# A mixture-of-experts tail in a two-layer decoder: outputs in a row per choice, w1 and w3 loaded per tile, the last batch in two parts

## The chip, the cores and the metric

The kernel runs on one core of a Trainium2 chip. The metric is the time of one execution on the device in microseconds (us); several runs are made, and their median counts. Of one further execution there is a hardware profile with every instruction's start and duration. The engines are TensorE (PE; its weight loads are listed apart as PEld), VectorE (DVE), ScalarE (ACT), GpSimd (POOL) and SyncE (SP), which only issues transfers here. SP and POOL issue DMA transfers to 16 shared DMA engines.

## The reference, cut to what matters

The input is x of 4 batches by 256 tokens by 256 features, and a context of 4 by 1601 by 256. Two layers follow each other, each with self-attention, cross-attention and a feed-forward part, and each part ends with a residual and a layer norm. Layer 0 has a sliding window, softmax attention over the context, and a ternary feed-forward part. Layer 1 has causal attention (16 heads over a compressed key), a gated linear attention over the context, and a mixture of experts, which is where the change lies:

```python
x = x + moe(x); out = layernorm(x)

def moe(x):                                   # x: 1024 tokens x 256
    logits = 30 * tanh((x @ w_gate) / 30)     # 8 experts
    probs = softmax(logits)
    idx = top_k(probs, 2)
    weights = probs * one_hot(idx).sum(-2)
    out = 0
    for e in range(8):
        h = silu(x @ w1[e]) * (x @ w3[e])     # 256 -> 512 inner units
        out += (h @ w2[e]) * weights[:, e]    # 512 -> 256
    return out
```

All is float32. Only two of eight experts count for a token, so the kernel sorts tokens by expert and computes only those.

## The kernel before, in words

The program isn't written in the order in which it runs. Each operation is recorded with the data it reads and writes, an estimated duration and a priority; then a planner (`Loom.weave`, L301) takes, again and again, the operation that can start earliest by its estimates, and writes it out. So the order on every engine is fixed when the program is built, by estimated times (`LAT` and the `us` of each operation), by the number of buffers of each kind, and by `at_prio`. At run time each engine follows its own list in order, and waits where the data aren't there. Almost every instruction is recorded by a helper, so the profile has the helper's line: L253 for matmuls, L260 for transposes, L382 for DVE, ACT and POOL operations, L267 for plain transfers. The tile names tell them apart. [...]

The main loop (L1464) goes over the four batches b: `l1_attention(b)`, `l1_cross(b)`, then `route(b)`. Tokens are handled in tiles of 128 (two per batch). After three batches the first tables of expert tiles are made, and their tiles may start while the fourth batch is still being worked on. Routing and experts work as follows.

- `moe_prepare` (L1176) fills the DRAM table `lists` with padding. Each expert has 1024 places in it, each place two numbers: gate and token. It zeroes `xd` and `acc`, two DRAM copies of x with spare rows.
- `route(b)` (L1227) writes x of the batch to `xd` and to `acc`, computes the gate (`wgate`), picks the two best, finds each token's place in its expert's list with five small matmuls against a triangular and an all-ones matrix (`ahead`, `onesb`: the rank), and scatters the entries with four indirect transfers on POOL (`enter`, L1212, `lists<-entry`).
- `tile_table(n, taken)` (L1287) computes on DVE which expert and which 128 rows of `lists` each of the next n tiles has. `EARLY` is 5 (the full tiles that must exist after three batches), `LATE` is 18 (all that can be left). Places that no token took are padding, and their rows go to spare rows.
- `expert_tile(i, tab)` (L1337) does one tile of 128 rows. SP reads the row number from the table and fetches the entries (`mine<-lists`, L1346). POOL gathers the 128 rows of x (`xg<-xd`, L1349). PE transposes them (2 transposes, `xgT`). Then xgT is the stationary side and w1, w3 (`w`, a slice of `w13` picked by a register) the moving side: 4 matmuls of 512 columns into two banks. ACT takes tanh of the first and DVE multiplies up to `eh`, 128 tokens by 512 units. PE transposes eh (4 transposes, `ehT`), multiplies with w2 (4 matmuls of 256 columns), DVE applies the gate (`ey`), and POOL adds the rows into `acc` in DRAM with an indirect transfer that adds (`acc<-ey`, L1357).
- At the end each batch's rows of `acc` are read back (L1482), normalised and written to `out`.

A float32 matmul is two instructions in the profile, each with a weight load of its own; a float32 transpose is one. Weights w1, w3 of all experts (8.4 MB) are loaded once into `w13` by 16 transfers, w2 (4.2 MB) once into `w2e`. The order of the adds into `acc` comes from the framework: two transfers that write the same DRAM tensor wait for each other unless they are declared independent, as the `enter` scatters are.

Of the kernel before, what the change touches and what calls it, by code (L numbers as in the profile page):

```python
# [175 lines left out]
class Loom:  # L176
# [62 lines left out]
    @contextmanager  # L239
    def piece(self, us, claims=(), ins=(), what=""):  # L240

        self.cur = ([], [], list(ins))
        yield
        fns, outs, ins = self.cur
        self.cur = None
        self.op({"PE": (us, us, lambda: [f() for f in fns])}, outs, ins, claims, what=what)
# [54 lines left out]
    def weave(self):  # L301
# [11 lines left out]
        while left:  # L313
# [22 lines left out]
            if op.size is not None:  # L336
                self.free["DMA"] = max(self.free["DMA"], at + us) + op.size / self.RATE
                op.end, op.engine = self.free["DMA"] + op.land, "DMA"
# [70 lines left out]
def decoder(ctx: ExitStack, tc: tile.TileContext, a: dict, out: bass.AP):  # L409
# [23 lines left out]
    down = scope("left", [even], on=experts)  # L433
# [15 lines left out]
    p6w, p6d = experts.pool("p6w"), down.pool("p6d")  # L449
# [138 lines left out]
    def normalise(x):  # L588
        mv = tiny((P, 2, 2), "mv")
        for t in range(2):  # L590
            st = tiny((P, 6), "st")
            k.vector.bn_stats(st, x[:, t, :])
            k.vector.bn_aggr(mv[:, t, :], st)
        rstd = tiny((P, 2), "rstd")
        k.gpsimd.tensor_scalar(rstd, mv[:, :, 1], 1e-5, None, ALU.add)
        k.gpsimd.tensor_tensor(rstd, rstd, mhalf, ALU.pow)
        for t in range(2):
            k.vector.tensor_scalar(
                x[:, t, :], x[:, t, :], mv[:, t, 0:1], rstd[:, t : t + 1], ALU.subtract, ALU.mult
            )  # L600

    def norm(b, x):

        normalise(x)
        xt = xpool.tile((P, 2, S), F32, "xt")
        ps = bank((P, 2, 2, P))
        for t in range(2):
            with piece(0.22, [xt], what="norm"):
                for c in range(2):
                    turn(ps[:, c, t, :], x[:, t, c * P : (c + 1) * P], ident)  # L610
        evac(xt.rearrange("p c (t q) -> p c t q", t=2), ps)
        X[b], XT[b] = x, xt
# [12 lines left out]
    def project_out(pool, x_new, t, x_old, o, wo, gate=None):  # L625
# [8 lines left out]
        else:  # L634
            k.vector.scalar_tensor_tensor(oT, gate[:, :, t * P : (t + 1) * P], 1.0, pt, ALU.add, ALU.mult)
# [16 lines left out]
    def l0_attention(b):  # L652
# [11 lines left out]
        for i in range(3):  # L664
            pv = bank((P, D))
            with piece(0.86, what="v"):
# [67 lines left out]
    def feature_map(pool, dst, ps, n, width, bufs=2):  # L734

        e = pool.tile((P, 512), F32, "fm", bufs=bufs)[:n, :width]
        k.scalar.activation(e, ps, AF.Exp)
# [314 lines left out]
    def l1_attention(b):  # L1052
# [16 lines left out]
        def four(q4):  # L1069

            ps = project_in(XT[b], lambda c, j: m_w[:, c, 2 * q4 + j, :], [qeT], "q")
            evac(qeT[:, 2 * q4 : 2 * q4 + 2, :], ps)
            aT0 = pool.tile((P, 2, 2, S), F32, "aTa")
            aT1 = pool.tile((P, 2, 2, P), F32, "aTb")
            for t in range(2):
# [4 lines left out]
                with piece(0.65 if t == 0 else 1.15, [at, aT0, aT1], what="scores"):  # L1080
# [15 lines left out]
                for kc in range(t + 1):  # L1096
# [4 lines left out]
                    dst = aT0[:, :, :, t * P : (t + 1) * P] if kc == 0 else aT1  # L1101
                    evac(dst, pt.rearrange("p (u i) q -> p u i q", u=2))

            po = bank((P, 2, S))
            with piece(1.42, what="pv"):
                for u in range(2):
                    half = slice(64 * u, 64 * u + 64)
                    mm(po[half], ctk[:, 0, :], aT0[:, u], True, False, skip_group_check=True)
                for u in range(2):
                    half = slice(64 * u, 64 * u + 64)  # L1110
                    mm(po[half, :, P:], ctk[:, 1, :], aT1[:, u], False, True, skip_group_check=True)
            evac(qeT[:, 2 * q4 : 2 * q4 + 2, :], po)

        for q4 in range(4):
            four(q4)
        xn = new_x()
        for t in range(2):
            py = bank((P, D))
            with piece(3.46, [xn], what="out"):
                for i in range(8):  # L1120
                    mm(py, qeT[:, i, t * P : (t + 1) * P], w2o[:, i, :], i == 0, i == 7)
            k.vector.tensor_tensor(xn[:, t, :], py, X[b][:, t, :], ALU.add)
        norm(b, xn)


    def l1_cross(b):
        pool = p5
        qf = pool.tile((P, 2, S), F32, "qf", bufs=1)
        pq = project_in(XT[b], lambda c, j: wqg[:, 0, c, j * P : (j + 1) * P], [qf], "q")
        feature_map(pool, qf.rearrange("p j q -> p (j q)"), pq.rearrange("p j q -> p (j q)"), P, 512, 1)  # L1130

        gate = pool.tile((P, 2, S), F32, "gate", bufs=1)
        pg = project_in(XT[b], lambda c, j: wqg[:, 1, c, j * P : (j + 1) * P], [gate], "gate")
        for j in range(2):
            k.scalar.activation(gate[:, j], pg[:, j], AF.Tanh, bias=bg[:, j : j + 1], scale=0.5)
        xn = new_x()
        for t in range(2):
            pn = bank((P, H, 17))
            o = pool.tile((P, H, 16), F32, "o")
            with piece(0.47, [o], what="kvs"):  # L1140
                for j in range(2):
                    mm(
                        pn[:, 8 * j : 8 * j + 8, :].rearrange("p h e -> p (h e)"),
                        qf[:, j, t * P : (t + 1) * P],
# [9 lines left out]
            project_out(pool, xn, t, X[b], o.rearrange("p h e -> p (h e)"), wxo, gate)  # L1154
        norm(b, xn)
# [8 lines left out]
    EARLY = -(-(2 * 3 * S - NE * (P - 1)) // P)  # L1164
    LATE = 2 * T // P + NE - 1 - EARLY
# [6 lines left out]
    lists = in_dram((LISTS, 2), "lists", I32)  # L1172
    xd = in_dram((T + P, D), "xd")
    acc = in_dram((T + P, D), "acc")

    def moe_prepare():  # L1176
# [9 lines left out]
        pad = tmp.tile((P, n, 2), I32, "pad", bufs=1)  # L1186
        k.gpsimd.memset(pad, 0)
        k.gpsimd.tensor_copy(pad[:, :, 1], w)
# [368 lines left out]
```

## Time and profile before

| | us |
|---|---|
| median of 3 runs (lowest, highest) | 734.64 (733.61, 734.69) |
| the profiled execution | 731.26 |
| its span, first to last instruction | 729.5 |
| PE busy in the span | 672.8 |
| DVE, ACT, POOL busy | 438.5, 302.6, 158.3 |
| expert tiles on PE, first to last | 551 to 708 |

The span is shorter than the execution's time by what lies before the first and after the last instruction. In the page's row of forty slices one slice is 18.2 us, and a digit is the busy share in tenths. PE is counted busy while matmuls are in flight, so its share tells where it stands still, and not how well it is used. [...] the pace is read from the distance between starts: 0.43 us for an instruction of 512 columns, 0.216 for 256, 0.109 for a transpose of 128. The DMA share is that of 16 engines, and GB/s what they moved.

### The profile page before, as it was taken

The numbers are of one execution on the slowest core, as the hardware profiler recorded it, in microseconds if no ns is written. First come the engines' busy times: TensorE is split into PE (matmuls) and PEld (weight loads), VectorE is DVE, ScalarE is ACT, GpSimd is POOL, SyncE is SP. The second block draws the span as 40 slices with busy tenths as digits, with TensorE's granted clock in tenths as the row PEclk, the third lists the DMA queues.
The fourth block names the chain that finished last, engine by engine and source line by source line (L and its number), as shares of the span: only waits on it lengthen the run. The fifth ranks groups of instructions, "written<-read, shape, count | busy, mean of one in ns | idle before, by whom it ended". The sixth has DMA issues, their size and how long they took to land.

```text
span 729.5 us, 11204 instructions
## 1 busy us (share of the span) xinstructions
PE 672.8 (92%) x3920; PEld 490.8 (67%) x3920; DVE 438.5 (60%) x1067; ACT 302.6 (41%) x931; POOL 158.3 (22%) x190
## 2 busy tenths in 40 slices
PE   7999999999999999999899999999977959999970
PEld 5778787678867786767676777777654635665640
DVE  4899886334493535665999877887754513333323
ACT  2868664211232224343467765656611202222210
POOL 3220324022100000000121010303122456522232
PEclk9999999999999999999999999999999989999995
DMA  9901212538632230000203900003601143312214
GB/s 307 341 18 59 92 35 87 173 128 273 219 115 91 91 122 1 1 0 1 53 1 115 347 1 30 1 30 62 199 2 37 30 56 90 59 21 23 23 22 123
DMA packets 51819, 63.39 MB, mean 87 GB/s; under 512 B 7758, under 2 KB 41684, under 8 KB 51764
## 3 DMA queue, kind: packets, MB, share of 16 engines
q1 hardware_dynamic: 46836, 56.63, 23.9%
q0 software_dynamic: 4928, 6.05, 5.3%
q8 instruction: 32, 0.52, 0.3%
q14 instruction: 23, 0.19, 0.1%
HBM read 54.05 MB, written 8.61 MB: 86 GB/s over the span
## 4 chain that ended last, share of the span: by engine, by line
PE 73%; DVE 13%; DMA 5%; ACT 4%; issue 2%; POOL 1%; SPq 0%; POOLq 0%; DVEq 0%; ACTq 0%
PE bank L253 65%; PE bank L260 8%; DVE at L382 3%; ACT at L382 3%; DMA acc<-ey,mine 2%; DVE nm L382 2%; DVE x L382 2%; DVE h L382 1%; DVE as L382 1%; DMA lists<-entry,rowi 1%; DMA xg<-xd,mine 1%; DVE st L382 1%; DMA x<-acc 1%; POOL rstd L382 1%; DMA wqkv<-in_wqkvT 0%
## 5 line engine op out<-in xcount | busy, mean ns | idle before, releaser
L382 ACT ACTIVATE at<-at,nm 128x128 f32<-128x128 f32 (+1 forms) x256 | 106.3, 418 | 23.5 <-DVE nm L382 22.9
L253 PE MATMUL bank<-w,xgT 128*128 x184 | 85.0, 608 | 0.5 <-ACT xgT L382 0.5
L260 PE MATMUL bank<-ident,at 128*128 128x128 f32 (+1 forms) x440 | 60.4, 275 | 1.1 <-DVE at L382 0.4
L253 PEld LDWEIGHTS bank<-w,xgT 128*128 128x128 f32 x184 | 35.0, 197 | 37.1 <-issue 36.0
L260 PEld LDWEIGHTS bank<-ident,at 128*128 128x128 f32 (+1 forms) x440 | 50.7, 141 | 13.0 <-issue 4.8
L382 POOL TENSOR_SCALAR rstd<-mv 128x2 f32<-128x2 f32 x24 | 6.3, 263 | 244.2 <-DVE mv L382 226.1
L253 PE MATMUL bank<-V,aT 128*128 128x256 f32 (+1 forms) x240 | 55.2, 380 | 1.4 <-DVE o L382 1.4
L253 PE MATMUL bank<-KT,qT 128*128 128x512 f32 (+1 forms) x128 | 53.8, 554 | 0.0
L253 PEld LDWEIGHTS bank<-V,aT 128*128 128x128 f32 (+1 forms) x240 | 45.0, 190 | 11.6 <-issue 4.4
L1357 POOL DMA_INDIRECT acc<-ey,mine x23 | 36.1, 1569 | 72.7 <-DVE ey L382 42.1
L253 PE MATMUL bank<-kf,V 128*128 128x256 f32 (+1 forms) x208 | 49.9, 382 | 1.1 <-DVE kf L382 1.1
L382 DVE TENSOR_REDUCE nm<-at 128x4 f32<-128x512 f32 x64 | 50.7, 809 | 0.5
L253 PE MATMUL bank<-wkv,KT 128*128 128x256 f32 (+1 forms) x208 | 49.7, 383 | 0.0
L382 ACT ACTIVATION_READ_ACCUMULATOR at<-at,nm 128x1 f32 x256 | 48.4, 189 | 0.0
L253 PE MATMUL bank<-w2e,ehT 128*128 x184 | 43.9, 385 | 2.9 <-ACT ehT L382 2.8
L382 POOL TENSOR_TENSOR at<-at,rs 128x512 f32<-128x512 f32 (+1 forms) x17 | 20.3, 1191 | 111.0 <-DVE rs L382 70.0
L253 PEld LDWEIGHTS bank<-kf,V 128*128 128x128 f32 (+1 forms) x208 | 38.5, 190 | 7.7 <-DVE kf L382 2.3
L382 ACT COPY aT<-bank 128x512 f32<-128x512 f32 (+2 forms) x57 | 29.1, 540 | 33.3 <-PE bank L260 33.0
L253 PEld LDWEIGHTS bank<-wkv,KT 128*128 128x128 f32 (+1 forms) x208 | 37.7, 186 | 7.5 <-issue 1.9
L253 PEld LDWEIGHTS bank<-w2e,ehT 128*128 128x128 f32 x184 | 34.0, 190 | 12.3 <-ACT ehT L382 4.4
L382 DVE TENSOR_TENSOR at<-at,rs 128x512 f32<-128x512 f32 (+1 forms) x47 | 39.2, 834 | 1.0
L382 ACT ACTIVATE eh<-bank 128x512 f32<-128x512 f32 x23 | 13.7, 597 | 59.4 <-PE bank L253 59.4
(248 smaller groups left out, 1252.0 us busy)
## 6 DMA issues: line engine op xcount, KB each, us to landing
w<-in_w SPq DMA_DIRECT2D x16, 512.0 KB, 9.3
KT<-in_ctxT SPq DMA_DIRECT2D x6, 1024.0 KB, 6.2
V<-in_ctx SPq DMA_DIRECT2D x6, 1024.0 KB, 7.5
w2e<-in_w SPq DMA_DIRECT2D x8, 512.0 KB, 9.4
KT<-in_ctxT SPq DMA_DIRECT2D x6, 577.0 KB, 4.7
V<-in_ctx SPq DMA_DIRECT2D x6, 512.0 KB, 4.1
wq<-in_w1qT SPq DMA_DIRECT2D x8, 256.0 KB, 4.8
wo<-in_w1o SPq DMA_DIRECT2D x8, 256.0 KB, 3.1
```

Of the source, the lines that this page charges most:

```text
L253: lambda: self.nc.tensor.matmul(real(o), real(lhsT), real(rhs), start=real(start), stop=stop, **kw)
L260: fns.append(lambda: self.nc.tensor.transpose(real(o), real(x), real(ident)))
L382: return getattr(engine, method)(*[real(x) for x in args], **{k: real(x) for k, x in kw.items()})
L1357: nc.gpsimd.indirect_dma_start(out=acc.real(), out_offset=bass.IndirectOffsetOnAxis(ap=ids.real(), axis=0), in_=y.real(), in_offset=None, ...
```

## The change

- An expert's output isn't added in DRAM any more. `yd` has a row for each token and choice (2 x 1024 rows, and one for each padding place). An entry of `lists` has a third number, that row. `expert_tile` scatters `ey` to those rows (`scatter`, called "give"), and the transfers are declared independent of each other. `acc` is gone. x stays in SBUF, and at the end each batch reads two blocks of `yd` (`back`, four buffers) and adds them to x on DVE before it is normalised.
- The inner units lie on the rows: w1 and w3 are the stationary side, in pieces of 128 units, and xgT the moving side, 128 columns. The result is h with units on the partitions, which is what the w2 matmul needs, so the four transposes and their evacuation go.
- w1 and w3 of a tile's expert are loaded for each tile, by SP with a register from the table, into one of four buffers (`wt`). `w13` and its 16 loads are gone; w2 stays loaded once, and its pool no longer waits for the attention's pool, so it comes earlier.
- `EARLY` becomes a list: 5 tiles after three batches and 2 more after the first half of the last batch; `LATE` becomes 16. For that the last batch goes through `l1_attention`, `l1_cross` and `route` in two halves of 128 tokens; `l1_attention` is a generator that yields after each half. The scatter of a half's entries is two transfers.
- `piece` gets an argument `over`: the matmuls of layer 0's v wait in the plan for the earlier readers of the v buffer they are evacuated to. The planner's estimate for small transfers (under 0.3 MB) changes. Both alter the order only.

The diff, cut to its core:

```diff
-    def piece(self, us, claims=(), ins=(), what=""):
+    def piece(self, us, claims=(), ins=(), over=(), what=""):
...
+        read = [o for v in over for _, o in v.buf.reads]
+        self.op({"PE": (us, us, lambda: [f() for f in fns])}, outs, ins, claims, after=read, what=what)
...
-                self.free["DMA"] = max(self.free["DMA"], at + us) + op.size / self.RATE
-                op.end, op.engine = self.free["DMA"] + op.land, "DMA"
+
+                begin, took = at + us, op.size / self.RATE
+                self.free["DMA"] = max(self.free["DMA"], begin) + took
+                if op.size < 0.3:
+                    behind = self.free["DMA"] - took > begin
+                    op.end = min(self.free["DMA"], begin + (2 * took + 1.0 if behind else took)) + op.land
+                else:
+                    op.end = self.free["DMA"] + op.land
+                op.engine = "DMA"
...
-    EARLY = -(-(2 * 3 * S - NE * (P - 1)) // P)
-    LATE = 2 * T // P + NE - 1 - EARLY
+    EARLY = [-(-(2 * n - NE * (P - 1)) // P) for n in (3 * S, T - P)]
+    EARLY[1] -= EARLY[0]
+    LATE = 2 * T // P + NE - 1 - sum(EARLY)
...
-    lists = in_dram((LISTS, 2), "lists", I32)
+    lists = in_dram((LISTS, 3), "lists", I32)
     xd = in_dram((T + P, D), "xd")
-    acc = in_dram((T + P, D), "acc")
+    yd = in_dram((2 * T + LISTS, D), "yd")
...
+    def scatter(dst, row, src, us, land, what):
+
+
         def emit():
             k.hold_order(False)
             d = nc.gpsimd.indirect_dma_start(
-                out=lists.real(),
+                out=dst.real(),
                 out_offset=bass.IndirectOffsetOnAxis(ap=row.real(), axis=0),
-                in_=entry.real(),
+                in_=src.real(),
                 in_offset=None,
             )
-            tc.declare_no_dep(d.ins, group="entries", reason="no two of them have a row in common")
-            tc.add_to_no_dep_group("entries", d.ins)
+            tc.declare_no_dep(d.ins, group=what, reason="no two of them have a row in common")
+            tc.add_to_no_dep_group(what, d.ins)
...
-        def add_up():
-            nc.gpsimd.indirect_dma_start(
-                out=acc.real(),
-                out_offset=bass.IndirectOffsetOnAxis(ap=ids.real(), axis=0),
-                in_=y.real(),
-                in_offset=None,
-                compute_op=ALU.add,
-            )
...
+        def weights():
+            expert(nc.sync)
+            for j, w in enumerate(("w1", "w3")):
+                nc.sync.dma_start(
+                    out=wt.real()[:, j],
+                    in_=a[w][bass.ds(reg[nc.sync], 1), :, :].rearrange("o (c p) n -> p (o c) n", p=P),
+                )
+
+        entry = p5.tile((P, 3), I32, "mine", bufs=LATE)
         k.op({"SP": (1.1, 1.1, fetch)}, [entry], [lists, tab], size=0.05, land=2.2, what="fetch")
-        ids, gate = entry[:, 1:2], entry[:, 0:1].bitcast(F32)
-        xg = pool.tile((P, D), F32, "xg", bufs=10)
+        wt = p6w.tile((P, 2, 2, EI), F32, "wt", bufs=4)
+        k.op({"SP": (1.6, 1.6, weights)}, [wt], [tab], size=8e-6 * D * EI, what="weights")
+        gate, ids, slots = entry[:, 0:1].bitcast(F32), entry[:, 1:2], entry[:, 2:3]
+        xg = p5.tile((P, D), F32, "xg", bufs=6)
...
-        with piece(3.45, [h], ins=[w13], what="tile"):
+
+        h = pool.tile((P, EI // P, P), F32, "eh")
+        pa = [bank((P, EI // P, P)), bank((P, EI // P, P))]
+        with piece(3.52, [h], what="tile"):
             for j in range(2):
-                for c in range(2):
-                    mm(
-                        pa[j], xgT[:, c, :], lambda j=j, c=c: w13.real()[:, bass.ds(reg["e"], 1), j, c, :].squeeze(1),
-                        c == 0, c == 1,
-                    )
+                for m in range(EI // P):
+                    for c in range(2):
+                        mm(pa[j][:, m], wt[:, j, c, m * P : (m + 1) * P], xgT[:, c, :], c == 0, c == 1)
...
-        hT = pool.tile((P, 4, P), F32, "ehT")
-        ph = bank((P, 4, P))
-        with piece(0.44, [hT], what="tile"):
-            for c in range(4):
-                turn(ph[:, c, :], h[:, c * P : (c + 1) * P], ident)
-        evac(hT, ph)
...
-        k.op({"POOL": (1.65, 1.65, add_up)}, [acc], [y, ids], size=0.13, what="add up")
+        scatter(yd, slots, y, 1.0, 2.0, "give")
...
-    w13 = p6w.tile((P, NE, 2, 2, EI), F32, "w13")
-    for e in range(NE):
-        k.dma_start(w13[:, e, 0], rows(a["w1"][e]))
-        k.dma_start(w13[:, e, 1], rows(a["w3"][e]))
-    w2 = p6d.tile((P, NE, 4, D), F32, "w2e")
+    w2 = p6w.tile((P, NE, 4, D), F32, "w2e")
...
     for b in range(B):
         at_prio(7, b)
-        l1_attention(b)
-        at_prio(6, b)
-        l1_cross(b)
-        if b == B - 1:
-            at_prio(8)
-            tab, taken = tile_table(EARLY, None)
-            for i in range(EARLY):
-                expert_tile(i, tab)
-        at_prio(6, b)
-        route(b)
+        for ts, x, xt in l1_attention(b):
+            at_prio(6, b)
+            if ts[0] == 0:
+                xn, xnt = p5.tile((P, 2, D), F32, "xl", bufs=B), new_xt()
+            l1_cross(b, ts, x, xt, xn, xnt)
+            if b == B - 1:
+                at_prio(8)
+                n = EARLY[ts[0]]
+                tab, taken = tile_table(n, taken)
+                for i in range(n):
+                    expert_tile(i, tab)
+            at_prio(6, b)
+            route(b, ts, xn, xnt)
+            at_prio(7, b)
+        X[b] = xn
     at_prio(8)
-    tab, _ = tile_table(LATE, taken)
+    tab, _ = tile_table(LATE, taken, True)
     for i in range(LATE):
         expert_tile(i, tab)
     for b in range(B):
-        x = new_x()
-        k.dma_start(x, acc[b * S : (b + 1) * S, :].rearrange("(t p) d -> p t d", p=P))
+        x = X[b]
+        for e in range(2):
+            y = p6.tile((P, 2, D), F32, "back", bufs=4)
+            row0 = e * T + b * S
+            k.dma_start(y, yd[row0 : row0 + S, :].rearrange("(t p) d -> p t d", p=P))
+            k.vector.tensor_tensor(x, x, y, ALU.add)
         normalise(x)
```

The core of the split in `l1_attention` is this loop, where the earlier kernel has `four(q4)` for both halves at once:

```python
        for ts in ((0,), (1,)) if b == B - 1 else ((0, 1),):
            for q4 in range(4):
                four(q4, ts)
            ...
            norm_into(xn, xt, ts)
            yield ts, xn, xt
```

## The prediction

> **What bounds the kernel now.** I read the page first (busy shares, the forty slices), then the chain that ended last, then tables by stage of the last third, and last the timelines of PE and POOL there.
>
> ```profile
> PE 672.8 (92%) x3920; PEld 490.8 (67%) x3920; DVE 438.5 (60%) x1067; ACT 302.6 (41%) x931; POOL 158.3 (22%) x190
> PE   7999999999999999999899999999977959999970
> DMA  9901212538632230000203900003601143312214
> ```
>
> PE is the bound nearly everywhere: 73% of the chain is PE work, and up to 533 us PE lacks only some 16 us, 5 of them waiting for the first weights. So a gain must shorten PE's own work or fill its holes. Two holes are left: slices 29 to 32 (529 to 602 us) and the last one and a half. The table by stage places them. Columns: window, its length, busy us (instructions) of PE, PEld, DVE, ACT, POOL, granted clock, DMA share, GB/s.
>
> ```profile
> 400.00:404.00 4.00, 4.00 (x26) 2.75 (x24) 3.79 (x7) 2.83 (x11) 0.00 (x0) 1.00 1.05 386
> 585.00:590.00 5.00, 3.23 (x16) 2.31 (x14) 1.26 (x3) 0.59 (x1) 1.34 (x1) 1.00 0.53 26
> 590.00:595.00 5.00, 0.00 (x0) 0.00 (x0) 0.00 (x0) 0.00 (x0) 2.58 (x2) 0.86 0.31 27
> 595.00:600.00 5.00, 3.09 (x5) 1.47 (x6) 0.00 (x0) 0.37 (x1) 3.24 (x3) 0.50 0.40 65
> 610.00:700.00 90.00, 89.56 (x337) 56.24 (x336) 29.70 (x49) 20.58 (x41) 31.44 (x24) 1.00 0.24 35
> 706.00:730.00 24.00, 1.99 (x8) 1.44 (x8) 6.86 (x25) 0.06 (x1) 6.57 (x10) 0.65 0.36 99
> ```
>
> From 610 to 700 PE is full: the expert tiles are purely PE-bound. Around 590 it stands still and then runs at half clock. What it waits for (start, duration, engine, line, operation, idle time before and its releaser):
>
> ```profile
> 586.91 1.99 PE L253 MATMUL bank<-w2e,ehT 128*128 x8 [0.68 <-ACT ehT L382]
> 596.45 0.66 PE L260 MATMUL bank<-ident,xg 128*128 128x128 f32 x2 [7.54 <-DMA xg<-xd,mine]
> 597.57 5.08 PE L253 MATMUL bank<-w,xgT 128*128 x8 [0.46 <-ACT xgT L382]
> 584.75 1.59 POOL L1357 DMA_INDIRECT acc<-ey,mine  x1 [0.30 <-DVE eh L382]
> 591.48 1.56 POOL L1357 DMA_INDIRECT acc<-ey,mine  x1 [5.14 <-DMA acc<-ey,mine]
> 593.34 1.02 POOL L1349 DMA_INDIRECT xg<-xd,mine  x1 [0.31 <-issue]
> ```
>
> The last batch's routing (rank matmuls at 577.6) must be scattered to the lists, land, be fetched and gathered before a late tile can start at 596.5, 19 us later; five early tiles don't cover it. POOL makes it worse: each add into acc waits for the add before, and the gathers queue behind.
>
> [...]
>
> ```profile
> 197.01 0.53 PEld L253 LDWEIGHTS bank<-wkv,gT 128*128 128x128 f32 x4
> 197.46 0.53 PEld L253 LDWEIGHTS bank<-ones,kacc 128*128 128x128 f32 x4
> ```
>
> Four loads in 0.45 us, 0.112 each, with 128 moving columns behind each, and 0.11 even with one column. [...] here it was granted 0.50 after 7.5 us, and that w pass took 5.08 us where a warm one takes 3.60. [...]
>
> **The change part by part.** The sum is against the profiled execution's 731.3 us.
>
> 1) *Units on the rows.* A tile on PE now: 2 transposes 0.22; w1 and w3 as 8 instructions of 0.43 (3.44); 4 transposes of eh 0.44; w2 8 x 0.216 = 1.73: 5.83 us. (17 w passes and 18 of everything else make 101 us; 604 to 705 is 101.) After, w1/w3 are the stationary side: 16 matmuls of 128 columns, two passes each, 32 x 0.111 = 3.55, and the four transposes and their evacuation (0.59 us, mostly on ACT) go: 5.50 us. 23 tiles x 0.33 = **-7.6 us**. [...]
>
> 2) *The last batch in two parts, 5+2 early and 16 late tiles.* PE's columns stay the same: causal attention and l1_cross work on 128 rows twice instead of 256 once. Extra small instructions on DVE, ACT and POOL hide under PE; DVE is 24 of 33 us busy from 500 to 533. In the built order of the changed kernel the last rank matmul is followed on PE by 3 w1/w3 blocks after its own tile's w2 chain: w2 x5 (8.6), w x3 (10.6), transposes: about 20 us before the first late gather is needed. The chain it covers shrinks: two scatters instead of four (-2.5) and no add to wait for, some 16 us, plus 2 for queueing. Its SP order has a cost: a weight load that waits for a free buffer, then the fetch. So the hole goes: 0.68 + 7.54 + 0.46 + 0.66 us idle and 1.5 slow = **-10.8 us** (bounds: -11 to 0).
>
> 3) *Weights per tile.* Each tile loads 1.05 MB, 24 MB in all instead of 8.4 once. The 400 to 404 row moved the same w1/w3 rows at 386 GB/s: 2.7 us per tile against 5.5 of PE, with four buffers, so in steady state it hides. SP needs about 1.05 us for a fetch and 1.6 for two loads with their register read (0.5 each when not held up): 2.7 of 5.5. If the cover went, a tile would run at DMA's pace. At the start it doesn't hide: fetches 1 to 4 stand behind weight loads, so I follow the order. With the third batch's rank done at 0, first rows are at PE at 17.4 as now (533.3 to 550.7); tile 2's rows, needed early in tile 1, come at about 25.5 where PE is ready at 24.7; tile 4's gather stands on POOL behind a give (which needs ey of tile 0, at 31.3) and two list scatters, and lands at 38.7 where PE asks at 37.3. The lists of part one land at 40.5, the next fetch follows. **+2.5 us** for these stalls (0 to +10). Loads of w2 move earlier, into the quiet 390 to 420: nothing.
>
> 4) *Rows in yd.* Scatters carry no wait on each other. In steady state the adds were hidden (PE full), so nothing but what 2) took. SP loses the waits on acc.
>
> 5) *The end of PE.* Now from the last w pass (701.6) to the last ey (starts 708.15) is 6.5 us, with two idle bits before w2. After: tanh 0.6, two DVE steps of 0.69 and hops, 2.4 us, then 1.73 and 0.2: 4.4. Of the 2.1 saved, 0.9 are transposes counted in 1): **-1.2**.
>
> 6) *The tail.* Now:
>
> ```profile
> 708.15 0.48 DVE L382 TENSOR_SCALAR ey<-bank,mine 128x256 f32<-128x256 f32 x1 [2.68 <-PE bank L253]
> 710.20 1.55 POOL L1357 DMA_INDIRECT acc<-ey,mine  x1 [2.91 <-DMA acc<-ey,mine]
> 713.95 1.92 SPq L267 DMA_DIRECT2D x<-acc  x4
> 716.63 0.76 DVE L382 BATCH_NORM_STATS2 st<-x 128x6 f32<-128x256 f32 x2 [8.00 <-DMA x<-acc]
> ```
>
> Last ey at 708.6, end at 729.5: 20.9 us. After: issue 0.3; scatter 3.6 (unseen; a gather lands in 2.8, an add in 3.8: bounds 2.8 to 5.4, a list scatter's median); SP 0.4; first row block 2.7; DVE, 7.7 us from 716.6 to 724.3, now with eight adds of 128x512 (0.68 us for such a step at 512.8) = 5.4 more, minus some 0.8 of gaps they fill; then 5.2 from the last DVE step to the end. 24.5: **+4.0** rounded up for eight loads through four buffers (bounds +1 to +6).
>
> 7) *The rest.* A planner lays out the whole program, and `over` and a new DMA estimate change its order from the first layer on. With PE nearly full there, I take 0, -4 to +4.
>
> Sum: -7.6 -10.8 +2.5 -1.2 +4.0 = -13.1, so 718.2 for a profiled execution. The profiled one was 3.4 under the median of its runs (734.64), so the median after: **721.6 us**.
>
> **Rivals.** *The hole stays* (15%): the late weight load heads SP's queue, waits for tile 3's buffer, and with scatters behind gathers on POOL the chain again outlasts the seven early tiles. For it: SP and POOL are strictly in order here, as 591.48 shows. Against: about 4 us of slack by my count. Price: the 10.8 comes back in the main: 728 to 733 us.
>
> *Better than that* (14%): the start stalls vanish and the tail's adds hide under landing loads; 2.5 + 3 less, and 2 to 3 from a better early order: 711 to 714.
>
> *The weights become the bound* (12%): gathers, gives and fetches share the engines, and the tile's pace becomes its 1.05 MB. Against: 386 GB/s seen, four buffers. It decides from 5.50 + 13.1/23 = 6.07 us per tile, 173 GB/s, on; at 150 GB/s a tile takes 7.0 and the kernel gets 34 us longer: about 756 us. A landing time doubled by contention with the buffer freed late would do the same.
>
> *It doesn't do what it says* (under 1%): gives still in series. The built order shows no wait of one give on another's landing.
>
> **How the numbers follow.** Forecast 57%, 714 to 728 us; rivals as above; 2% no change. About 0.2% is what a measurement of this kernel can tell from none, so faster means under 733.2: 57 + 14 + 14 (the standing hole, nearly all of it) = 85%; within 2%; slower 13%. The range leaves out the weights case and the outer edges: 711 to 732. The forecast's own: 714 to 728.
>
> **What would show it.** w1/w3 in 32 passes of 0.11 us and a tile period of 5.5 (step 1); no PE wait over 2 us on xg between the early and late tiles, clock 1.0 there (2); small waits on xg or wt in the first four tiles, and wt landing under 8 us (3); no wait of a give on a give (4); last ey to end about 25 us, DVE busy 12 of it (6). A PE wait on wt in the steady stage, or passes over 0.125 us, would make the prediction wrong.

## The result, and the profile after

| | before | after |
|---|---|---|
| median us (lowest to highest, runs) | 734.21 (733.61 to 734.69, 4) | 746.29 (745.44 to 749.01, 4) |
| the profiled execution, its span | 731.26, 729.5 | 749.01, 747.2 |

After/before is 1.0179, 95% interval 1.0159 to 1.0199: 1.8% slower. 721.6 us was predicted; it is 25 us more, and on the other side. The profiled executions differ by 17.7 us of span, where the working had -13.1: 30.8 us are to be found.

The page of after, its busy PE and the slices of PE and of the transfers (18.7 us each):

```profile
PE 677.9 (91%) x4407; PEld 539.0 (72%) x4411; DVE 447.8 (60%) x1118; ACT 292.3 (39%) x916; POOL 152.8 (20%) x199
PE   5899899999999999999899899999976888999960
DMA  9910121436732341000100600000003648776424
```

The digits where the prediction looked (the last ten) aren't much worse than before. The first is: 5 where it was 7. Two milestones, read from the first and last start of a tile's instructions, split the span: the last matmul of layer 0's feed-forward part (`wq,hqT`), and the last `ey` on DVE. Between them PE's time is split by two-us windows of the stage table: not busy is idle; busy times one minus the granted clock is what the lower clock costs; the rest is work.

| us | before | after |
|---|---|---|
| start to the last `wq,hqT` | 393.7 | 409.0 |
| of it idle / lost to the clock | 11.6 / 0.0 | 19.6 / 6.0 |
| from there to the last `ey` | 314.4 | 312.7 |
| of it work | 285.9 | 277.7 |
| of it idle / lost to the clock | 23.7 / 4.8 | 24.2 / 10.9 |
| last `ey` (its start) to the end | 21.4 | 25.5 |

So 15.3 of the 17.7 us arise in layer 0, before the attention, routing and experts of layer 1 that the change is about; 4.1 are the tail; the middle, where 8.2 us of work went, won only 1.7.

**The early part.** The timeline of PE, after, and the stage table of the same microseconds, before and then after (columns as in the prediction):

```profile
12.58 1.33 PE L255 MATMUL bank<-kT,qT 32*128 32x256 f32 x24
19.82 6.50 PE L255 MATMUL bank<-xt,wqkv 128*128 128x256 f32 x16 [5.91 <-DMA xt<-in_xT]
```
```profile
14.00:19.00 5.00, 5.00 (x43) 3.88 (x36) 4.01 (x8) 2.34 (x11) 0.00 (x0) 1.00 1.09 354
19.00:27.00 8.00, 6.83 (x56) 4.98 (x55) 6.50 (x15) 6.63 (x29) 2.35 (x3) 1.00 1.07 390
```
```profile
14.00:19.00 5.00, 0.00 (x0) 0.00 (x0) 4.83 (x8) 0.00 (x0) 0.00 (x0) 0.97 1.09 363
19.00:27.00 8.00, 7.18 (x20) 5.88 (x21) 0.75 (x1) 3.39 (x16) 0.00 (x0) 0.59 1.07 389
```

After, PE stands 5.91 us for the transposed x of the second batch, and then does its 16 matmuls in 6.50 us, 0.41 each where a warm one of 256 columns takes 0.216: 20 instructions in eight us where before had 56. A second wait that before doesn't have follows: 2.05 us at 35.29, for `at` on POOL.

**The tiles, the late rows and the tail** (steady stage, timeline of PE there and at the first late tiles, and the last `ey` with what follows on its chain):

```profile
640.00:715.00 75.00, 75.00 (x571) 71.87 (x570) 25.55 (x42) 12.11 (x27) 23.31 (x25) 1.00 0.63 213
723.00:747.00 24.00, 0.00 (x0) 0.00 (x0) 11.46 (x32) 0.00 (x0) 5.30 (x9) 0.55 0.44 137
```
```profile
644.86 7.31 PE L255 MATMUL bank<-xgT,wt 128*128 128x128 f32 x64
661.41 7.31 PE L255 MATMUL bank<-xgT,wt 128*128 128x128 f32 x64
...
604.88 0.43 PE L262 MATMUL bank<-ident,xg 128*128 128x128 f32 x2 [0.28 <-DMA xg<-xd,mine]
633.32 0.44 PE L262 MATMUL bank<-ident,xg 128*128 128x128 f32 x2 [2.21 <-DMA xg<-xd,mine]
```
```profile
721.67 0.48 DVE L391 TENSOR_SCALAR ey<-bank,mine 128x256 f32<-128x256 f32 x1 [1.24 <-PE bank L255]
722.43 0.96 POOL L1258 DMA_INDIRECT yd<-ey,mine  x1 [0.77 <-DVE ey L391]
724.97 6.97 SPq L269 DMA_DIRECT2D back<-yd  x8
727.79 1.50 DVE L391 TENSOR_TENSOR xl<-xl,back 128x512 f32<-128x512 f32 x2 [5.63 <-DMA back<-yd]
```

Three tiles take 661.41 - 644.86 = 16.55 us, 5.52 each, with PE 100% busy while the transfers, the tiles' weights among them, move 213 GB/s. The wait of 7.54 us for the late rows is gone; 2.21 is the longest one left. From the end of the last `ey` (722.15) to the end are 25.0 us, and DVE is busy 11.5 of the last 24, where the prediction had 12.

**The middle.** What it won at 585 to 600 it lost again in waits that before doesn't have (PE, after):

```profile
423.84 1.06 PE L262 MATMUL bank<-ident,at 128*128 128x128 f32 x8 [2.47 <-ACT at L391]
...
542.53 1.06 PE L262 MATMUL bank<-ident,at 128*128 128x128 f32 x8 [1.13 <-DVE mv L391]
544.85 1.11 PE L262 MATMUL bank<-ident,xl 128*128 128x128 f32 x4 [1.25 <-DVE xl L391]
...
564.88 1.08 PE L262 MATMUL bank<-ident,at 128*128 128x128 f32 x4 [2.87 <-DVE upto L391]
579.62 0.41 PE L262 MATMUL bank<-ident,x 128*128 128x128 f32 x2 [2.81 <-DVE upto L391]
```
```profile
545.00:547.00 2.00, 2.00 (x10) 1.45 (x12) 1.66 (x3) 1.00 (x4) 0.00 (x0) 0.50 0.39 131
566.00:574.00 8.00, 6.90 (x25) 5.17 (x26) 3.85 (x26) 1.93 (x5) 1.53 (x2) 0.50 0.13 26
```

No wait here is over 3 us, and yet each group of them is followed by some us at a clock of 0.50 (426 to 428, 545 to 547, 566 to 574 and 582 to 584 us). The largest group lies in the last batch, whose second half stands behind DVE: `upto` is a step of the tile table, in DVE's queue among the softmax of the half batch.

### The profile page after: what moved, and what is told of

Same layout as the page of the kernel before. It is cut to its first block, busy times and chain, and to the rows that moved or that the text cites. A ratio compares the mean times of both kernels' runs of the same rounds, so it can differ in the third digit from the quotient of the medians.

```text
span 747.2 us, 12375 instructions
## 1 busy us (share of the span) xinstructions
PE 677.9 (91%) x4407; PEld 539.0 (72%) x4411; DVE 447.8 (60%) x1118; ACT 292.3 (39%) x916; POOL 152.8 (20%) x199
## 4 chain that ended last, share of the span: by engine, by line
PE 74%; DVE 10%; DMA 5%; POOL 3%; issue 3%; SPq 2%; ACT 2%; POOLq 0%; DVEq 0%; ACTq 0%
PE bank L255 66%; PE bank L262 9%; DVE at L391 4%; SPq L269 2%; DVE nm L391 2%; POOL lists L1258 1%; ACT at L391 1%; DMA xg<-xd,mine 1%; POOL rstd L391 1%; DMA xt<-in_xT 1%; DMA trig<-in_rope 1%; DMA back<-yd 1%; DVE xl L391 1%; DVE x L391 1%; DVE st L391 0%
## 5 line engine op out<-in xcount | busy, mean ns | idle before, releaser
L255 PE MATMUL bank<-xgT,wt 128*128 128x128 f32 x736 | 87.1, 279 | 0.5 <-ACT xgT L391 0.5
L255 PEld LDWEIGHTS bank<-xgT,wt 128*128 128x128 f32 x736 | 86.6, 196 | 1.3 <-ACT xgT L391 0.7
L391 POOL TENSOR_SCALAR rstd<-mv 128x2 f32<-128x2 f32 (+1 forms) x26 | 8.4, 322 | 218.1 <-DVE mv L391 190.2
L391 DVE TENSOR_REDUCE nm<-at 128x4 f32<-128x512 f32 (+1 forms) x64 | 50.5, 809 | 0.3
L391 POOL TENSOR_TENSOR at<-at,rs 128x512 f32<-128x512 f32 (+1 forms) x18 | 22.5, 1250 | 129.3 <-DVE rs L391 114.8
L391 ACT COPY aT<-bank 128x512 f32<-128x512 f32 (+2 forms) x59 | 29.9, 544 | 37.7 <-PE bank L262 37.4
L255 PE MATMUL bank<-w2e,eh 128*128 x184 | 43.3, 380 | 0.0
L391 DVE SCALAR_TENSOR_TENSOR eh<-eh,bank 128x512 f32<-128x512 f32 x23 | 15.8, 686 | 36.2 <-ACT eh L391 36.2
L1258 POOL DMA_INDIRECT yd<-ey,mine x23 | 22.7, 985 | 71.0 <-DVE ey L391 55.7
```

The source lines that it names most:

```text
L255: lambda: self.nc.tensor.matmul(real(o), real(lhsT), real(rhs), start=real(start), stop=stop, **kw)
L391: return getattr(engine, method)(*[real(x) for x in args], **{k: real(x) for k, x in kw.items()})
L1258: d = nc.gpsimd.indirect_dma_start(out=dst.real(), out_offset=bass.IndirectOffsetOnAxis(ap=row.real(), axis=0), in_=src.real(), in_offset= ...
```

## The experiments

Ratios are to the kernel before, run beside each kernel on the same chip; 0.1% is 0.73 us. The medians of before itself range from 731.2 to 736.0 us over the chips used, so verdicts go by ratios and the traces are read for places. "Order" means here all that the planner decides: the order on each engine, and also the engine itself for some copies and products (thr02 has 1114 instructions on DVE and 920 on ACT, iota2 1109 and 925).

### Is the early loss the planner's estimate?

The new estimate treats every transfer under 0.3 MB as one that needn't wait its turn: `begin + 2 x took + 1.0 + land`, with 0.262/0.25 = 1.05 and a `land` of 1.6, 4.7 us after its issue. That covers the gathers of 0.13 MB, and also the x loads of 0.262 MB. In the run, the second batch's x was issued at 12.06 us behind the context's loads, and PE got it at 19.82, 7.8 later. The context's loads were issued from 3.34 us on, before this one, and the transfers moved 363 GB/s from 14 to 19 us; what held the x back among them the trace doesn't name. By its estimate the planner put this batch's matmuls right behind the first batch's scores, and the context's first keys (`wkv,KT`) after them, although their data were there: thr02 runs them at 13.55 without a wait. Three kernels: thr02 moves the bound,

```diff
-                if op.size < 0.3:
+                if op.size < 0.2:
```

est_old takes the estimate of before for all sizes and keeps `over`:

```diff
-                begin, took = at + us, op.size / self.RATE
...
+                self.free["DMA"] = max(self.free["DMA"], at + us) + op.size / self.RATE
+                op.end, op.engine = self.free["DMA"] + op.land, "DMA"
```

and before_est_new is the kernel before with the new estimate (bound 0.3) and `over`, and nothing else of the change.

> The changed kernel, with one number changed: the planner's new estimate for transfers holds under 0.2 MB instead of 0.3, so it still covers the gathers and scatters of 0.13 MB and no longer the 0.26 MB loads of x and of weights at the start. No instruction is added or removed; only the order is laid out anew. Theory A (step 7 failed: with the bound at 0.3 the planner believes that batch 1's x lands early, puts its q, k, v matmuls fifth on PE, and PE stands 5.9 us for x there and starts cold): the first layer-0 cross-attention matmul comes at about 186 instead of 198.7, and the time is 10 to 15 us lower, 731 to 736. Theory B (the early loss has nothing to do with the estimate; it comes from other pools or the wait of the v matmuls, argument over): within 3 us of the changed kernel's 746.

> The changed kernel with the planner's estimate for transfers as it was before the change, for all sizes; the argument over stays. Theory A: the early part is as in the run with the bound at 0.2 MB, first layer-0 cross-attention matmul at about 186; the expert part, whose order the estimate was made for, may be laid out worse: 731 to 740. Theory B: 746, as the changed kernel.

> The kernel before, with the planner's new estimate (bound 0.3 MB) and the argument over, and nothing else of the change: the same instructions in another order. Theory A: it loses by itself what the changed kernel loses early, first layer-0 cross-attention matmul at about 198 instead of 185.9, and the time is 10 to 18 us over the kernel before: 744 to 752. Theory B: 734, as before.

| | ratio (95%) | first `wqk` matmul | last `wq,hqT` |
|---|---|---|---|
| before | 1 | 185.9 | 393.7 |
| after | 1.0179 (1.0159 to 1.0199) | 198.7 | 409.0 |
| thr02 | 1.0054 (1.0036 to 1.0073) | 186.1 | 394.6 |
| est_old | 1.0094 (1.0061 to 1.0126) | 186.3 | 394.9 |
| before_est_new | 1.0165 (1.0128 to 1.0202) | 196.9 | 403.9 |

PE in thr02, and in before_est_new, in the same place:

```profile
13.55 5.45 PE L255 MATMUL bank<-wkv,KT 128*128 128x256 f32 x24
20.12 1.99 PE L255 MATMUL bank<-kf,V 128*128 128x256 f32 x8 [1.12 <-DVE kf L391]
```
```profile
19.66 5.67 PE L254 MATMUL bank<-xt,wqkv 128*128 128x256 f32 x15 [4.62 <-DMA xt<-in_xT]
```

Theory A stands from both sides: one number undoes the early loss (14.4 us to the last `wq,hqT`, 1.25% of the time), and the planner's edits alone, put into the kernel before, bring it: 1.65%, nearly as much as the whole change. est_old keeps `over` and has no early loss, so `over` isn't its cause. What is left in thr02's span are 4.0 us of tail and 0.9 early, of which the middle, 311.8 us long, gives back 2.6. est_old isn't better than thr02, so no harm of the new estimate for the 0.13 MB gathers shows; one order of each can't exclude it.

### What the split is worth

```diff
-for ts in ((0,), (1,)) if b == B - 1 else ((0, 1),):
+for ts in ((0, 1),):
-EARLY = [... for n in (3 * S, T - P)]
+EARLY = [... for n in (3 * S,)]
```

> The changed kernel without its last batch in two parts: one pass of 256 tokens, 5 early and 18 late tiles as in the kernel before; the rest stays, the early order too. Theory C (splitting costs more in front of the tiles, in DVE work and a longer way from rank to first rows, than the hole it fills): the way from the third batch's rank to the first rows falls from 25 to about 17, the hole before the late tiles is back (8 to 11 us), and the time is within 3 us of the changed kernel's 746. My step 2 as predicted (splitting is worth 10.8 and costs nothing): about 755 to 757.

1.0319 (1.0291 to 1.0346): 1.4% or 10.3 us over after. In this order theory C falls, and step 2's 10.8 for the split was about right. But the hole it fills isn't the 7.54 us of before (PE, then SP's queue, of no_split):

```profile
599.04 0.17 PE L255 MATMUL bank<-hotb,ahead 128*128 128x8 bf16 x1
622.67 0.66 PE L262 MATMUL bank<-ident,xg 128*128 128x128 f32 x2 [16.28 <-DMA xg<-xd,mine]
```
```profile
606.31 2.72 SPq L1413 DMA_DIRECT2D wt<-in_w  x4
609.89 2.63 SPq L1397 DMA_DIRECT2D mine<-lists  x3
```

```profile
617.42 0.98 POOL L1400 DMA_INDIRECT xg<-xd,mine  x1 [8.73 <-DMA wt<-in_w]
```

From the last rank matmul to the first late rows are 23.6 us instead of 18.8. Two tiles' weights stand on SP's queue ahead of the fetches, and the profile puts the end of the gather's wait, on POOL, down to their landing: from the first fetch to the gather are 7.5 us where before has 4.0, and from the gather to PE 5.3 where before has 3.1. So the weights lengthen the hole that the split then fills.

### The tiles alone

tiles_only is the kernel before with units on the rows and weights per tile; acc, the last batch in one part and the old estimate stay, and so does PE's order up to the first expert tile.

> The kernel before, with two parts of the change alone: inner units on the rows, and w1 and w3 loaded per tile (w2's pool with them). The adds into acc, the last batch in one part and the old estimate stay; up to the first expert tile PE's order is the one of the kernel before. Steps 1, 3 and 5 as predicted: PE's work falls by 8 us and the time by 8 to 10 (ratio about 0.988). Theory F (fetches of list rows stand on SP's queue behind weight loads, and are late where no early tile covers them): PE's work falls by 8, but the way from the last rank matmul to the first late rows grows from 18.8 to about 24 us, and 3 to 5 us are left (ratio 0.993 to 0.996).

1.0081 (1.0057 to 1.0106), 0.8% slower. PE's work in the middle fell from 285.9 to 278.3, as step 1 has it, but idle rose from 23.7 to 33.8 and the loss to the clock from 4.8 to 9.7 (SP's queue, what SP's fetches waited for from 560 to 605, then PE):

```profile
566.67 17.63 SPq L1370 DMA_DIRECT2D wt<-in_w  x8
590.02 6.19 SPq L1345 DMA_DIRECT2D mine<-lists  x6
```
```profile
SPq L1345 <- DMA lists<-entry,rowi: 4.9, 1, 4.9
```
```profile
602.59 0.66 PE L260 MATMUL bank<-ident,xg 128*128 128x128 f32 x2 [9.03 <-DMA xg<-xd,mine]
617.36 6.10 PE L253 MATMUL bank<-xgT,wt 128*128 128x128 f32 x32 [6.87 <-DVE xgT L382]
```

Theory F has the direction (the way from the last rank, at 572.7, to the late rows grew to 29.9 us), but neither the size nor the whole mechanism: SP is through with four tiles' weights at 584.3, and the late fetch then still waits 4.9 us for the list scatters, the last of which POOL had issued at 579.6. From that scatter's issue to the fetch's are 10.4 us, where before, with no weights under way, has 5.9 (583.49 to 589.38). In 585 to 590 the transfers moved 190 GB/s and their engines were busy all the time (share 1.08); whether that made the scatters land late was not tested. What held DVE's copy of `xgT` before 617.36 the profile doesn't name; that 6.87 stays open. In this order, without the split, weights per tile cost more than the 8 us they make possible.

### Rows in yd undone

acc_again is thr02 with the adds into `acc` and one read back per batch.

> The changed kernel with the planner's bound at 0.2 MB, and rows in yd undone: experts' outputs are added into acc in DRAM, one after the other, and read back once at the end. Steps 4 and 6 as predicted (yd costs 4 us in the tail and saves nothing in the steady tiles): 25 us from the last ey to the end become 21, and the time is 4 us under the run with the bound at 0.2 MB (ratio about 1.000). Rival (serial adds stand in front of the late tiles' scatters and gathers on POOL, which yd took away): the tail gains 4, and the wait for the late rows grows by 4 or more; ratio 1.005 to 1.012.

1.0022 (1.0006 to 1.0038), where thr02 has 1.0054 and the same order on another chip (two_as_four, below) 1.0023. So yd shows neither cost nor gain here; but acc_again is another order too, and orders differ by more than the 4 us in question, so this is no price of yd. Neither expectation holds (two adds and the stage table of 640 to 660, then the last `ey`, the adds after it, the read back):

```profile
641.77 1.58 POOL L1411 DMA_INDIRECT acc<-ey,mine  x1 [6.63 <-DVE ey L391]
...
683.56 1.55 POOL L1411 DMA_INDIRECT acc<-ey,mine  x1 [3.77 <-DVE ey L391]
```
```profile
640.00:660.00 20.00, 20.00 (x156) 19.01 (x155) 6.40 (x12) 2.39 (x4) 7.78 (x6) 1.00 0.89 271
```
```profile
705.37 0.48 DVE L391 TENSOR_SCALAR ey<-bank,mine 128x256 f32<-128x256 f32 x1 [3.97 <-DMA acc<-ey,mine]
...
714.85 1.55 POOL L1411 DMA_INDIRECT acc<-ey,mine  x1 [2.97 <-DMA acc<-ey,mine]
718.59 1.91 SPq L269 DMA_DIRECT2D x<-acc  x4
```

At the end an add takes some 4.4 us from one to the next, and three of them stand after the last `ey`: from its start to the end are 29.0 us where thr02 has 25.4. With tiles of 5.5 us no queue should form at that pace; but the eight adds from 641.77 to 683.56 start 6.0 us apart, while weights arrive (271 GB/s in 640 to 660), so they fall behind. Whether the loads slow the adds was not tested. The tail of 20.9 that step 6 compared with stems from a kernel with slower tiles and no weights under way.

### Is the rest order, too?

thr02 has PE waits that before lacks at 406 to 411. The table of the two row numbers (`places`) was then filled by two iotas (instructions on POOL that write running numbers) instead of four; this puts PE's order there back as in before.

```diff
-for e in range(2):
-    for j in range(2):
-        iota(places[:, :, e, j], P, base=e * j * T, cm=1)
+for j in range(2):
+    k.gpsimd.iota(places[:, :, :, j], [[P, T // P], [j * T, 2]], base=0, ...)
```

> The changed kernel with the planner's bound at 0.2 MB, and one thing more: the table that holds each token's two row numbers (places) is filled by two POOL iotas instead of four. This moves the planner's order on PE at the start of layer 1's attention (394 to 416 us) back to the one that the kernel before has. Theory A2 (the 2.5 us that PE stands for ACT at 409 and the half clock after it are nothing but a worse order there): the first matmul with layer 1's output weights comes at about 412 instead of 415.9, and the time is 3 to 5 us under the run with the bound at 0.2 MB, about equal to the kernel before (ratio 0.999 to 1.001). Rival (the hole comes from the loads of w2, which now run in 400 to 410): no change, ratio 1.005.

0.9868 (0.9836 to 0.9899): 1.9% under thr02, not 0.5%, and faster than the kernel before. The wait of 2.47 us is gone, but most of the gain lies later, in the last batch. Two instructions of 0.14 us on POOL can hardly do that, the order can; four runs were to tell:

> The changed kernel with two iotas instead of four, and the planner's bound left at 0.3 MB as changed. Theory A: the early loss stays whole, because batch 1's x is still planned too early: first layer-0 cross-attention matmul at about 198, and the ratio to before is about 0.987 + 0.018 = 1.003 to 1.008. Rival (the two iotas fewer repair the order altogether): 0.987.

> As iota2, with the planner's estimate for every DVE instruction raised by 5 ns (0.155 to 0.160 us fixed part). No instruction is changed; some 270 of 1200 rows of PE's order stand otherwise. Theory O (the order is the largest single term here, and any small edit draws a new one): the time moves by 3 to 9 us, upwards from the good draw, ratio 0.991 to 0.999. Rival (iota2 is good because of what it removes, POOL work in front of layer 1): within 2 us of iota2.

> As iota2, and the third batch's four list scatters on POOL come after the layer-norm power of the last batch's first half instead of before it; the lists come up to 2 us later for that, and the planner lays out the end of the last batch anew. Theory P (the power stands behind four scatters of 1.3 us on POOL, and holds up DVE, whose queue holds the tile table and a softmax): from the third rank to the first rows PE's waits of 6.8 us for DVE fall to about 3, and the time by 2 to 4 us against iota2. Theory G (half a batch has too little PE work to cover its own softmax and norm, whoever is first on POOL): within 1.5 us of iota2.

> As iota2, with the last batch in one part: 5 early and 18 late tiles. In the changed kernel's own order the split was worth 10 us by the ratios. If it is worth that whatever the order (step 2's mechanism: seven early tiles cover the way from the last rank to the first late rows): the wait for the late rows is back with 12 to 16 us and the ratio to before is 1.000 to 1.004. Rival (the split's own holes cost as much as the one it fills, once the order is good): within 4 us of iota2, ratio 0.987 to 0.992.

- iota2_03: 0.9993 (0.9971 to 1.0014), 1.25% over iota2, with 4.78 us of waiting for x at 19.64. The early loss is the same 1.25% in either layout, and adds to the rest.
- iota2_dve5ns: 0.9888 (0.9840 to 0.9937), as iota2. This fitted the rival, that the missing iotas did it.
- iota2_rstd_first: 0.9957 (0.9946 to 0.9969). The edit didn't reach its aim: indirect transfers are emitted outside the planned order, and the scatters still stand before the power. Only the order of the last batch differs, so theory P wasn't tested; as one more layout it costs 0.9%.

```profile
536.81 1.09 POOL L1262 DMA_INDIRECT lists<-entry,rowi  x1 [6.49 <-DVE nt L391]
...
548.99 0.58 POOL L391 TENSOR_TENSOR rstd<-rstd,mhalf 128x1 f32<-128x1 f32 x1
```

- iota2_no_split: 0.9928 (0.9906 to 0.9949). In this layout the split is worth 0.6%, 4.4 us, not 1.4%: between the two expectations.

What decided was to exchange order and iotas. In four_as_two the four iotas run but each pair is planned as one; in two_as_four two run, planned as four. All other instructions stand, on every engine, as in iota2 and thr02 respectively (in the traces PE's matmuls come in the same sequence).

> The changed kernel with the planner's bound at 0.2 MB and its four iotas, of which each pair is planned as one operation with the estimate of one iota of twice the width. So the four iotas run, but on every engine all other instructions stand in the order of iota2. Theory O (the order made iota2 faster): ratio to before 0.984 to 0.991, as iota2. Rival (the two iotas fewer did it): 1.003 to 1.008, as the run with the bound at 0.2 MB.

> The reverse: two iotas run, planned as four. On every engine all other instructions stand in the order of the run with the bound at 0.2 MB. Theory O: ratio 1.003 to 1.008. Rival: 0.984 to 0.991.

> The changed kernel with the bound at 0.2 MB, four iotas, and the planner's estimate for every DVE instruction raised by 5 ns: a third order of the same instructions (170 of 1200 rows of PE's order stand otherwise than with the bound alone). Theory O gives no value, only that it lies among the other orders, 0.987 to 1.010; a value that differs from 1.005 by more than 0.4% shows again that the order alone moves the time.

four_as_two has 0.9846 (0.9798 to 0.9894), two_as_four 1.0023 (1.0007 to 1.0038), thr02_dve5ns 0.9893 (0.9867 to 0.9919). The order does it, whichever iotas run. iota2 and four_as_two are faster than both kernels; iota2 stands to after as 0.9868/1.0179 = 0.969. PE's longest waits from 390 to 640 us (total, times, longest), two_as_four and then four_as_two:

```profile
PE bank L262 <- DVE upto L391: 6.9, 3, 2.9
PE bank L262 <- DVE xl L391: 2.8, 2, 1.5
PE bank L262 <- ACT at L391: 2.5, 1, 2.5
```
```profile
PE bank L262 <- DVE o L391: 2.7, 1, 2.7
PE bank L262 <- DVE ixf L391: 2.4, 1, 2.4
PE bank L262 <- DVE xl L391: 1.6, 2, 1.3
```

From the last `wq,hqT` to the last `ey` two_as_four takes 316.5 us, four_as_two 299.1, on the same chip: idle 24.3 against 14.6, lost to the clock 14.2 against 4.5, work 278.0 and 280.0. Before and after that stage they are within 1.3 us of each other. In the good order the third batch's rank comes at 532.9 and the last one at 576.7, in the other at 544.3 and 599.4. That the half batches' DVE steps are better covered by other matmuls there is a reading of the two timelines; which exchange of places does it was not tested.

All layouts of the changed kernel's instructions, two iotas apart:

| layout | ratio |
|---|---|
| as changed (bound 0.3 MB) | 1.0179 |
| est_old | 1.0094 |
| thr02; the same order again, two_as_four | 1.0054; 1.0023 |
| iota2_03 | 0.9993 |
| iota2_rstd_first | 0.9957 |
| thr02_dve5ns | 0.9893 |
| iota2_dve5ns | 0.9888 |
| iota2; the same order again, four_as_two | 0.9868; 0.9846 |

### A shorter table and tail

iota2_tri_pool makes the table's running sum of 2 DVE instructions instead of 8, and one of two adds per batch at the end on POOL.

> As iota2, with two shortenings: the running sum over experts in the tile table is one product with a triangle and one sum (2 DVE instructions instead of 8, three tables), and of the two adds per batch at the end one runs on POOL beside DVE. Expected: 1 to 2 us from the tables, where DVE holds up PE after the third rank, and 2 to 3 from the tail (last ey to end 22 to 23 instead of 25): ratio 0.981 to 0.985. Rival (the new plan or POOL's slower add takes it back): 0.986 to 0.995.

0.9912 (0.9877 to 0.9946), no better than iota2; the rival holds. POOL's add takes 1.25 us where DVE's takes 0.69, and DVE waits for it:

```profile
707.25 1.25 POOL L391 TENSOR_TENSOR xl<-xl,back 128x512 f32<-128x512 f32 x1 [4.30 <-DMA back<-yd]
708.53 0.69 DVE L391 TENSOR_TENSOR xl<-xl,back 128x512 f32<-128x512 f32 x1 [6.83 <-POOL xl L391]
```

The tail stayed at 25.8 us. What the table alone would bring can't be told, since its edit made another order (8.2 us of waits for `xg`).

## Why the prediction was wrong

**Step 7 failed** ("The rest": 0, -4 to +4). It named the cause, `over` and the new estimate, and then took PE's full slices as a reason that order can't cost much. Full slices say the reverse: there is no slack in which a transfer planned too early could hide. By itself the planner's edit costs 1.65% in the kernel before, and `over`, which step 7 names too, has no part in the early loss (est_old). The bound of 0.3 MB stands in the diff, and the x loads of 0.262 MB fall under it; the first rows of the changed kernel's order on PE would have shown what follows, a sum over the stages of before can't.

How much in all: as changed 1.0179, in the best order found 0.9846; the difference is 3.3%, 24.5 us, which step 7 had at nothing. 1.25% of it is the bound, the rest the order of the middle. In that order the change gives -1.5%, 11.3 us of 734.2, where the steps added up to -13.1. The sum of steps 1 to 6 lies inside that ratio's interval (-7.8 to -14.8 us), for an order that the changed kernel doesn't have. Much of that agreement is luck. 0.9846 belongs to the best of eight orders, while the kernel before stands in its own one, and how far its time moves between orders is not known (before_est_new, the only other one, is slower). The five orders with the bound at 0.2 MB average 0.993 (the two runs of one order taken as one value), or -5 us. And the terms of the middle were not each right:

- Step 1 (-7.6) and step 5 (-1.2): PE's work in the middle fell by 8.2 us in after and 8.3 in thr02 (4.8 at the least in the other orders of the table); 5.52 us per tile where 5.50 was worked out, and 3.7 us from the last w1/w3 pass to the last `ey` (718.01 to 721.67) where 4.4 was. Right in the main.
- Step 2 (-10.8): the hole went, as said, and removing the split costs 10.3 us. But "extra small instructions on DVE, ACT and POOL hide under PE" is wrong in the changed order: DVE's `upto`, `xl` and `mv` hold PE up, and the clock's loss doubles from 4.8 to 10.9. "DVE is 24 of 33 us busy" was a mean; a half batch needs DVE in one chain.
- Step 3 (+2.5): hidden in the steady stage, as said; the waits for rows are 0.28 us at 604.88 and 2.21 at 633.32, 2.5 together, the sum that was forecast, but not in the first four tiles, so the size is luck. The first rows reach PE 25.3 us after the third batch's rank (555.86 to 581.21, after) and not 17.4 as in the working; what that costs by itself was not measured. Step 3 left out that weights ahead of late fetches lengthen the very hole that step 2 fills, from 18.8 to 23.6 us (no_split). Step 2 should have been priced against that hole.
- Step 4 (0): right; no give waits for another.
- Step 6 (+4.0): 25.0 against 20.9, +4.1. Right against before, though with acc at the new pace the tail isn't shorter (acc_again).

None of the rivals was the one that came; a plan that makes PE wait in layer 0 was not among them, so the 13% for slower stood on the wrong mechanism. The range, 711 to 732, would have held iota2's and four_as_two's medians (724.97 and 722.27), not that of the changed kernel.

## What to carry to other kernels

Where a planner or scheduler lays out the program, an edit of its estimates is a change of the whole kernel: follow the order's first rows and ask of each transfer that it believes early whether the real queue delivers it then (here 4.7 us after its issue by the estimate, 7.8 in the run). Price a gain in the middle of such a kernel with the spread between orders, here 2.1% with one and the same estimate for transfers (0.9846 to 1.0054) and 3.3% in all, and try a few neutral edits, on the kernel before too, before judging a change by one layout. And when a change puts new transfers on a queue, count them in front of the latency-bound fetches that already use it (here the way to the first late rows was 23.6 us with them, in no_split, and 18.8 before).

## What the runs showed of the hardware

Short waits cost twice here. In after, waits of 1.13 and 1.25 us within 3.5 us were followed by a clock of 0.50 from 545 to 547, and the middle lost 10.9 us to the clock with no single wait over 3 us. Not every such pair was followed by it: waits of 0.68 and 1.35 us from 556.4 to 559.6 left the clock at 1.00. Over the middle the slow clock adds 20% of the idle time in before, where one wait of 7.54 us is a third of it, and 30 to 58% in the changed kernel's orders (four_as_two: 4.5 us lost beside 14.6 idle; two_as_four: 14.2 beside 24.3).

The indirect scatters to `yd` occupy POOL for 0.97 us (median of 23, after) and start 1.3 apart when nothing else holds them (631.71 and 633.01); an indirect add takes 1.55, and 4.3 to 4.6 from one to the next where each waits for the last (acc_again, from 683.56 on). POOL's float32 add of 128x512 took 1.25 us, DVE's 0.69 (iota2_tri_pool, 707.25 and 708.53).
